# Attention scores in runs of 3, 3 and 2 key tiles, with PSUM banks lent between scores and other products

## The chip, the cores and the metric

The kernel runs on one NeuronCore of a Trainium2 chip. The time is the device time of one execution in microseconds; a kernel is run several times and its median counts. The engines are TensorE (PE, with its weight loads shown apart as PEld), VectorE (DVE), ScalarE (ACT), GpSimd (POOL) and SyncE (SP), which here only issues DMAs. Each engine works through its own queue in order, and the queues meet at semaphores. TensorE writes to PSUM, which has eight banks; a bank holds 512 fp32 numbers in each of 128 partitions, and a [128, 2, 512] tile takes two banks.

## What is computed

Everything is fp32. With x of shape (4, 1024, 1024), a condition of shape (4, 1024) and 16 heads of 64 numbers:

```python
scale, shift = split(cond[:, None, :] @ W_emb + b_emb)
xn = rms_norm(x, g_norm) * (1 + scale) + shift
q, k, v = heads(xn @ W_qkv)                # each (4, 16, 1024, 64)
q, k = rms_norm(q, g_q), rms_norm(k, g_k)
attn = softmax(q @ k.T * 64 ** -0.5)       # over 1024 keys
o = attn @ v
x1 = x + (o + o @ W_out)
y = x1 + causal_conv(x1, taps=cond) + L1_cond_b   # 4 taps along the sequence
```

## The kernel before

**Units.** Attention is cut into 64 units, in the loop `for p in range(B * NB)` at the end of the kernel: a batch (4), a pair of heads (8) and a half of the queries (2 of 512). A unit has eight key tiles of 128 keys. For each tile `scores` multiplies keys and queries for both heads, which lie in the two halves of the PE's rows and run side by side (L688), into a [128, 2, 512] tile `s` of two banks. ScalarE copies it to SBUF as `sp` (L696; the pool of `sp` has nine buffers, so the copy of tile 1 waits until the unit before has used its own tile 0), and VectorE folds it into a running maximum `mx` (L705).

**Softmax of a unit.** `softmax` puts off the following steps by a planner's clock: GpSimd reduces `mx` over the partitions (L710), ScalarE writes the result to a PSUM tile `mbp` (L719), and then for each tile VectorE subtracts it (`shift`, L724), ScalarE takes the exponential and GpSimd adds to a sum (`weigh`, L728 and L730). One unit later `values` multiplies by v (L751, both heads side by side in the PE's columns, into the bank `pav`), and `finish` adds up the denominators (`tot`, L766), which go through DRAM to come back as one reciprocal a row (`spread`, `invert`, L784 to L799), with which `divide` scales the result (L806).

**Pieces.** All other work is a list of pieces for each unit, made by `between(p)`: seven products of the QKV projection (`piece`, L648; each is 8 matmul instructions of 384 columns, fp32 matmuls being issued as two; the projection is done in blocks with 7 products in place of 8, so VectorE adds each product to others when it empties it, L660 to L669), transposes of q and k (`qkt`, L506) and of the next batch's x (`xtp`, L312), and from unit 18 on the output projection of the batch before (`po`, L940, L995, L1009) and the transposes of its results (`otp`, L1056). A piece carries a planned time; `run` calls each, and `tick` moves the planner's clock on and issues what has become due. `need(key)` issues put-off steps of that key at once. What is issued in Python order is each engine's order (`manual_schedule`).

**Where pieces stand.** `split` takes pieces from the end of the list until 26 us of planned time (22 for the first 16 units) are together, to be run behind the unit's last scores; what is left goes into three stretches between the scores:

```python
unit.scores((0, 1))
if last is not None:
    need("exp", last.name)
    last.values(range(0, HT))
fill()
unit.scores((2, 3)); fill(); last.values(range(4, 6)); unit.scores((4, 5))
last.values(range(6, NT)); last.finish(); fill()
unit.scores((6, 7)); need("mx", unit.name); unit.softmax(); fill()
```

Only in units 24, 25, 40 and 41 is the list longer than that, and a timed piece (one QKV product, in 25 and 41 also two transposes) stands between the scores; everywhere else all timed pieces already stand behind the scores.

**PSUM.** The pool `ps_s` has two buffers of two banks for score tiles and `mbp`; `ps_m` has three single banks, taken in turn by every other product and transpose; `ps_a` has one bank for `pav`. That is all eight banks.

Of the kernel before, what the change touches and what calls it, by code (L numbers as in the profile page):

```python
# [21 lines left out]
def kernel(  # L22
# [53 lines left out]
    small = ctx.enter_context(tc.tile_pool(name="small", bufs=2))  # L76
    ps_s = ctx.enter_context(tc.tile_pool(name="ps_s", bufs=2, space=bass.MemoryType.PSUM))
    ps_m = ctx.enter_context(tc.tile_pool(name="ps_m", bufs=3, space=bass.MemoryType.PSUM))
    dram = ctx.enter_context(tc.tile_pool(name="dram", bufs=1, space=bass.MemoryType.DRAM))
# [62 lines left out]

    turn = [0]

    def evacuate(dst, src):

        turn[0] ^= 1
        if turn[0]:
            nc.scalar.copy(dst, src)
        else:  # L150
            nc.vector.tensor_copy(dst, src)

# [23 lines left out]
    for i, g in enumerate((g_q, g_k)):  # L176
        for h in range(2):
            nc.sync.dma_start(rows[R_GQ + i : R_GQ + i + 1, h * D : (h + 1) * D], g.rearrange("(o d) -> o d", o=1))
    cols_ps = ps_m.tile([P, 512], F32, tag="m", name="cols_ps")
    nc.tensor.transpose(cols_ps[:, :NR], rows, ident[:NR, :NR])  # L180
# [83 lines left out]
    class Chunk:  # L264
# [31 lines left out]
        def transposes(self, c):  # L296
            b, k, q = self.b, self.k, self.q
            need("xg", self.name)
            if c == 0:
# [9 lines left out]
                self.stores = [(rs[i // n][:, : min(n, 7 - i), :], i, min(i + n, 7)) for i in range(0, 7, n)]  # L309
            tp = ps_m.tile([P, 2, QN], F32, tag="m", name=f"xtp_{self.name}_{c}")  # L310
            for i in range(4):
# [69 lines left out]
    class Embed:  # L381
# [22 lines left out]
        def run(self):  # L404
            half = self.half
            ps = ps_m.tile([P, 512], F32, tag="m", name=f"mod_ps_{half}")[:, :QN]
            for k in range(NJ):
# [10 lines left out]

            mt = ps_m.tile([P, 512], F32, tag="m", name=f"modT_ps_{half}")[:, :QN]
            mt = mt.rearrange("p (i g b) -> p i g b", i=2, g=4)  # L420
# [27 lines left out]
    class Pair:  # L448
# [51 lines left out]
        def transposes(self, g, s):  # L500

            b, c = self.b, self.c
            need("qk", b, c, g)
            tp = ps_m.tile([P, HN], F32, tag="m", name=f"qkt_{b}_{c}_{g}_{s}")
            for i in range(HT):
                nc.tensor.transpose(  # L506
                    tp[:, i * P : (i + 1) * P], self.qk[g][:, i, s * P : (s + 1) * P], ident
                )
            tag = ("qT", "kT")[s]
            dst = apool.tile([P, HN], F32, tag=f"{tag}{c % 2}{g}", name=f"{tag}_{b}_{c}_{g}", bufs=1)  # L510
            if s:
                nc.scalar.activation(dst, tp, AF.Identity, scale=gqk)
            else:
                nc.scalar.copy(dst, tp)
            (self.qT, self.kT)[s][g] = dst
# [70 lines left out]
    class Double:  # L586
# [39 lines left out]
        def direct(self, c, q):  # L626

            a = self.a[(A11, A12)[c], q] = self.tile_a((A11, A12)[c], q)
            for k in range(KH):
                tp = ps_m.tile([P, 512], F32, tag="m", name=f"xtd_{c}_{q}_{k}")[:, :QN]  # L630
                for i in range(2):
# [6 lines left out]
        def piece(self, i):  # L638

            name, place, t = self.products[i]  # L640
            px, py = self.pairs
            pm = ps_m.tile([P, 512], F32, tag="m", name=f"pqkv_{self.n}_{name}_{t}")[:, :W3]
            w, a = self.w[name], self.a.get((place, t // 2))
# [33 lines left out]
    class Unit:  # L677
# [5 lines left out]
        def scores(self, kts):  # L683
            pr = self.pr
            for kt in kts:
                ps = ps_s.tile([P, 2, HN], F32, tag="s", name=f"s_{self.name}_{kt}")
                for h in range(2):
                    nc.tensor.matmul(  # L688
                        ps[:, h, :],
                        pr.kT[kt // HT][h * D : (h + 1) * D, kt % HT * P : (kt % HT + 1) * P],  # L690
# [4 lines left out]
                sp = apool.tile([P, 2, HN], F32, tag="sp", name=f"sp_{self.name}_{kt}", bufs=9)  # L695
                nc.scalar.copy(sp, ps)  # L696
                self.sp.append(sp)
# [19 lines left out]
        def broadcast(self):  # L717
            mb = ps_s.tile([P, 2, HN], F32, tag="s", name=f"mbp_{self.name}")
            nc.scalar.copy(mb, self.mb)  # L719
# [40 lines left out]
        def finish(self):  # L760
            b, c = self.pr.b, self.pr.c
            tot = ps_m.tile([P, HN], F32, tag="m", name=f"tot_{self.name}")
            for g in range(4):
# [13 lines left out]
            key = ("tot", self.name)  # L777
            defer(0.2, key, lambda: self.spread(tot))
            defer(8.0, key, self.invert)
# [117 lines left out]
    class Quad:  # L897
# [29 lines left out]
        def product(self, name):  # L927
# [9 lines left out]
            else:  # L937
                pm = ps_m.tile([P, 512], F32, tag="m", name=f"po_{b}_{j}_{name}")
            for k in range(KH):
# [23 lines left out]
    class Out:  # L963
# [27 lines left out]
        def residual(self, whole=False):  # L991

            self.pm = ps_m.tile([P, 512], F32, tag="m", name=f"po_{self.name}")
            for i in range(HT):
# [56 lines left out]
        def store(self):  # L1051
            b, j, half = self.b, self.j, self.half
            need("y", self.name)
            tp = ps_m.tile([P, 512], F32, tag="m", name=f"otp_{self.name}")
            for i in range(HT):
# [15 lines left out]
    TO_MAX, TO_SPREAD, TO_SHIFT, TO_EXP, STEP = 2.6, 6.5, 7.6, 1.3, 1.8  # L1071
    BEHIND = 26
    SHARES = (0.25, 0.5, 0.25)
    LEADS = ((11, 7), (10, 9))
    LEADS_LAST = ((11, 7), (10, 12))
    DIVIDE = 18.0
    STEP_FIRST = 1.6
    BEHIND_FIRST = 22.0
    LATER = ((0, 0), (4, 0))
# [174 lines left out]

    def cut(pieces, shares):

        ends = list(accumulate(shares))
        total = sum(t for t, _ in pieces)
        stretches, done = [[] for _ in shares], 0.0
        for t, step in pieces:  # L1260
            at = (done + t / 2) / max(total, 1e-9) * ends[-1]
            stretches[next((i for i, e in enumerate(ends) if at < e), len(ends) - 1)].append((t, step))
            done += t
        return stretches

    def run(pieces):
        for t, step in pieces:
            until = clock[0] + t
            step()
            if until > clock[0]:  # L1270
                tick(until - clock[0])

    def split(pieces, behind):

        left, n = behind, len(pieces)
        while n and left > 0:
            n -= 1
            left -= pieces[n][0]
        return cut(pieces[:n], SHARES) + [pieces[n:]]


# [41 lines left out]
    for p in range(B * NB):  # L1323
        unit = Unit(doubles[p // 4].pairs[p // 2 % 2], p % 2)
        stretches = split(between(p), BEHIND if p >= NB else BEHIND_FIRST)
        if p == B * NB - 1:


            gather(B - 1, 0)
            gather(B - 1, 1)  # L1330
            stretches = cut(between(p), SHARES) + [own]
        stretches = iter(stretches)

        def fill():
            run(next(stretches))

        unit.scores((0, 1))
        if last is not None:
            need("exp", last.name)
            last.values(range(0, HT))  # L1340
        fill()
        unit.scores((2, 3))
        fill()
        if last is not None:
            last.values(range(4, 6))
        unit.scores((4, 5))
        if last is not None:
            last.values(range(6, NT))
            last.finish()
        fill()  # L1350
        unit.scores((6, 7))
        need("mx", unit.name)
        unit.softmax()
        if last is not None:
            defer(2.7 if p > B * NB - 2 else DIVIDE, ("oT", last.pr.b, last.pr.c, last.half), last.divide)
        fill()
        last = unit
# [46 lines left out]
```

## Time and profile before

| what | us |
|---|---|
| median of the timed runs (3) | 2852.54 (2851.46 to 2853.9) |
| span of the profiled execution, first to last instruction | 2846.5 |
| median less span (what lies around the span) | 6.0 |
| PE busy (matmuls) | 2764.2, 97% |
| VectorE, ScalarE, GpSimd busy | 2161.3, 1541.5, 1345.1 |
| QKV products L648 | 1172.5 |
| scores L688, values L751 | 516.3, 486.5 |
| DMA, mean over the span | 179 GB/s |

The profile is of one execution, whose own time around its span is not recorded apart; the span is what its rows add up to. A busy PE counts modelled ends of pipelined matmuls, so the distance from one start to the next says more than a duration. A row of the timeline has the start, the time, the engine, the line, the operation, the tiles (out<-in), the count of merged instructions and, in brackets, the idle time before it and what ended it. A row of the waits has the total idle time, the number of waits and the longest. The clock that was granted to TensorE is 0.995 of full speed over the span.

### The profile page before, as it was taken

What the parts mean: (1) busy time and instruction counts of PE and PEld (TensorE: products, weight loads), DVE (VectorE), ACT (ScalarE), POOL (GpSimd) and SP (SyncE); (2) the same over time, 40 slices, a digit from 0 to 9 for tenths busy, and PEclk for the clock granted to TensorE, in tenths of its full rate; (3) what the DMA queues carried; (4) which work ended last, traced back from release to release, by engine and by line L of the source; (5) the groups of instructions that cost most, each with busy time, mean ns of one, the idle gap of its engine ahead of it and who ended that gap; (6) DMA issues with size and microseconds to landing.
All of it is one profiled execution on the core that took longest, in us unless ns stands there. A gap on an engine that the chain in (4) does not pass through costs nothing.

```text
span 2846.5 us, 31973 instructions
## 1 busy us (share of the span) xinstructions
PE 2764.2 (97%) x10581; PEld 1310.7 (46%) x10581; DVE 2161.3 (76%) x2579; ACT 1541.5 (54%) x2221; POOL 1345.1 (47%) x534
## 2 busy tenths in 40 slices
PE   6999999999999999999999999999999999999998
PEld 3544444444444444444444445445444444443344
DVE  4688887888888777777877777787877877687863
ACT  4255656655555556655555556665555545555532
POOL 2056554565654453553555355355445445554520
PEclk9999999999999999999999999999999999999999
DMA  9844555644565566665565556666556444533334
GB/s 318 280 168 145 193 174 184 211 152 169 174 196 159 174 196 205 214 229 164 162 207 186 165 178 212 203 218 198 163 202 211 141 130 159 167 109 96 118 108 118
DMA packets 416844, 509.40 MB, mean 179 GB/s; under 512 B 40816, under 2 KB 326824, under 8 KB 406952
## 3 DMA queue, kind: packets, MB, share of 16 engines
q1 hardware_dynamic: 416680, 507.36, 55.1%
q8 instruction: 85, 1.39, 0.2%
q14 instruction: 79, 0.65, 0.1%
HBM read 411.85 MB, written 95.40 MB: 178 GB/s over the span
## 4 chain that ended last, share of the span: by engine, by line
PE 78%; DVE 11%; DMA 4%; ACT 3%; issue 2%; POOL 2%; SPq 1%; DVEq 0%; ACTq 0%; POOLq 0%
PE pqkv_P L648 29%; PE pav L751 15%; PE s L688 15%; PE po L1009 5%; PE po_P L940 4%; PE po L940 4%; DVE sp L724 3%; DVE mx L705 3%; POOL sum L730 1%; PE qkt L506 1%; PE tot L766 1%; DMA scrR<-few 1%; DVE qk L498 1%; PE po L995 1%; ACT sp L696 1%
## 5 line engine op out<-in xcount | busy, mean ns | idle before, releaser
L648 PE MATMUL pqkv_P<-w_P,a 128*128 128x384 f32 x3456 | 1172.5, 490 | 15.5 <-issue 5.6
L730 POOL TENSOR_TENSOR sum<-sum,sp 128x1024 f32<-128x1024 f32 x384 | 956.8, 2492 | 36.5 <-ACT sp L728 5.7
L648 PEld LDWEIGHTS pqkv_P<-w_P,a 128*128 128x128 f32 x3456 | 639.4, 190 | 478.7 <-issue 69.2
L696 ACT COPY sp<-s 128x1024 f32<-128x1024 f32 x512 | 506.0, 1015 | 507.4 <-PE s L688 459.1
L705 DVE TENSOR_TENSOR mx<-mx,sp 128x1024 f32<-128x1024 f32 x384 | 518.9, 1351 | 170.9 <-ACT sp L696 143.8
L728 ACT ACTIVATE sp<-sp 128x1024 f32<-128x1024 f32 x512 | 531.8, 1055 | 204.6 <-DVE sp L724 201.3
L724 DVE TENSOR_TENSOR sp<-sp,mbp 128x1024 f32<-128x1024 f32 x512 | 604.2, 1210 | 19.3 <-ACT mbp L719 19.3
L710 POOL PARTITION_ALL_REDUCE mb<-mx x64 | 219.2, 3426 | 826.5 <-DVE mx L705 785.0
L688 PE MATMUL s<-qT,kT 64*128 64x512 f32 x2048 | 516.3, 620 | 21.8 <-DVE sp L724 17.0
L751 PE MATMUL pav<-sp,v 128*64 128x512 f32 x2048 | 486.5, 607 | 0.0
L730 POOL TENSOR_TENSOR sum<-sp,sp 128x1024 f32<-128x1024 f32 x64 | 151.5, 2367 | 485.6 <-ACT sp L728 232.9
L688 PEld LDWEIGHTS s<-qT,kT 64*128 64x128 f32 x2048 | 174.9, 186 | 314.8 <-issue 200.0
L751 PEld LDWEIGHTS pav<-sp,v 128*64 128x64 f32 x2048 | 131.2, 137 | 331.9 <-issue 322.2
L1045 DVE SCALAR_TENSOR_TENSOR y<-x,cols,y 128x512 f32<-128x512 f32 x192 | 224.3, 1173 | 47.9 <-ACT y L1033 43.3
L705 DVE TENSOR_TENSOR mx<-sp,sp 128x1024 f32<-128x1024 f32 x64 | 113.2, 1769 | 102.1 <-ACT sp L696 102.0
L667 DVE TENSOR_TENSOR qk<-u,pqkv_P 128x256 f32<-128x256 f32 x256 | 106.2, 415 | 77.9 <-PE pqkv_P L648 76.5
L1009 PE MATMUL po<-ob,wo 128*128 128x512 f32 x352 | 155.3, 593 | 0.0
L940 PE MATMUL po_P<-o_P,wq_P 128*128 128x512 f32 x320 | 143.9, 592 | 0.0
L498 DVE TENSOR_TENSOR qk<-qk,ms 128x1024 f32<-128x1024 f32 x64 | 129.7, 2047 | 0.0
L719 ACT COPY mbp<-mb 128x1024 f32<-128x1024 f32 x64 | 65.2, 1018 | 111.0 <-POOL mb L710 111.0
L940 PE MATMUL po<-o_P,wq_P 128*128 128x512 f32 x240 | 108.0, 592 | 0.0
L485 ACT ACTIVATE sq<-qk 128x512 f32<-128x512 f32 x128 | 76.7, 627 | 53.6 <-DVE qk L667 53.6
(94 smaller groups left out, 1730.7 us busy)
## 6 DMA issues: line engine op xcount, KB each, us to landing
a<-scrA SPq DMA_DIRECT2D x212, 512.0 KB
w_P<-scrB SPq DMA_DIRECT2D x64, 768.0 KB
o_P<-scrS SPq DMA_DIRECT2D x40, 1024.0 KB
w_P<-in_L_cond_W_qkv_dram SPq DMA_DIRECT2D x192, 192.0 KB
o_P<-scrO SPq DMA_DIRECT2D x30, 1024.0 KB
scrA<-r SPq DMA_DIRECT2D x28, 896.0 KB
wq_P<-scrW SPq DMA_DIRECT2D x70, 256.0 KB
xc<-in_x_dram SPq DMA_DIRECT2D x64, 256.0 KB
```

What stands on the lines that cost most here:

```text
L648: nc.tensor.matmul(pm, (chunk.r(place) if a is None else a[:, k, :])[:, t % 2 * P : (t % 2 + 1) * P], w[:, k, :], start=(k == 0), stop=(k ...
L688: nc.tensor.matmul(ps[:, h, :], pr.kT[kt // HT][h * D : (h + 1) * D, kt % HT * P : (kt % HT + 1) * P], pr.qT[self.half][h * D : (h + 1) * ...
L696: nc.scalar.copy(sp, ps)
L705: nc.vector.tensor_max(self.mx, self.mx if kt > 1 else self.sp[0], self.sp[kt])
L710: nc.gpsimd.partition_all_reduce(self.mb.rearrange("p h q -> p (h q)"), self.mx.rearrange("p h q -> p (h q)"), P, bass_isa.ReduceOp.max,)
L724: nc.vector.tensor_sub(self.sp[kt], self.sp[kt], self.mb)
L728: nc.scalar.activation(sp, sp, AF.Exp)
L730: nc.gpsimd.tensor_tensor(self.sum, self.sum if kt > 1 else self.sp[0], sp, ALU.add)
L751: nc.tensor.matmul(self.pav[h * D : (h + 1) * D, :], self.pr.v[kt // HT][:, kt % HT, h * D : (h + 1) * D], self.sp[kt][:, h, :], start=(kt ...
L940: nc.tensor.matmul(pm, self.w[name][:, k, :], self.o[name][:, k, :], start=(k == 0 and name not in ("P2", "P3", "P4")), stop=(k == KH - 1),)
L1009: nc.tensor.matmul(self.pm, self.w[kh][:, k % KH, :], oTs[b, k, half], start=False, stop=(k == NJ - 1),)
L1045: nc.vector.scalar_tensor_tensor(self.y, self.x1[:, k : k + HN], cols[:, r : r + 1], self.y, ALU.mult, ALU.add)
```

## The change

One pool `psum` with a tag for each bank or bank pair takes the place of `ps_s` and `ps_m`: pairs `s0` and `s1`, single banks `b0`, `b1` and `m`; `pav` keeps its own. Score tile kt uses `s1`, `b0`+`b1`, `s0` in turn; a tile in `b0`+`b1` is copied to SBUF by two ScalarE copies of 512 columns. `mbp` always uses `s0`. Scores are issued in runs of 3, 3 and 2, the values in two runs of 4, `need("exp", ...)` stands ahead of the first scores, and all pieces run behind the last scores. The other products take banks from a list in turn: behind the scores `m, s1, b0, b1` (a pair's first bank is used), during the scores only `m`, ahead of unit 0 also `s0`, and in the last unit without `m`; each change of list starts again at its first entry. `spread` (the copy of `tot` and its DMAs) is issued at once and not 0.2 us of planned time later. `split`, `cut` and the constants BEHIND, SHARES and BEHIND_FIRST go, and an unused helper with them.

```diff
-    ps_s = ctx.enter_context(tc.tile_pool(name="ps_s", bufs=2, space=bass.MemoryType.PSUM))
-    ps_m = ctx.enter_context(tc.tile_pool(name="ps_m", bufs=3, space=bass.MemoryType.PSUM))
+    psum = ctx.enter_context(tc.tile_pool(name="psum", bufs=1, space=bass.MemoryType.PSUM))
...
+    def double_bank(i, name):
+        return psum.tile([P, 2, 512], F32, tag=f"s{i}", name=name)
+    APART = ["m"]
+    FILL = ["m", "s1", "b0", "b1"]
+    ALL = FILL + ["s0"]
+    banks, at_bank = [ALL], [0]
+    def use_banks(some):
+        banks[0], at_bank[0] = some, 0
+    def bank(name):
+        tag = banks[0][at_bank[0] % len(banks[0])]
+        at_bank[0] += 1
+        if tag[0] == "s":
+            return double_bank(int(tag[1]), name)[:, 0, :]
+        return psum.tile([P, 512], F32, tag=tag, name=name)
...
-            pm = ps_m.tile([P, 512], F32, tag="m", name=f"pqkv_{self.n}_{name}_{t}")[:, :W3]
+            pm = bank(f"pqkv_{self.n}_{name}_{t}")[:, :W3]
...
-                ps = ps_s.tile([P, 2, HN], F32, tag="s", name=f"s_{self.name}_{kt}")
+                name = f"s_{self.name}_{kt}"
+                if kt % 3 == 1:
+                    ps = [psum.tile([P, HN], F32, tag=f"b{h}", name=f"{name}_{h}") for h in range(2)]
+                else:
+                    whole = double_bank((kt + 1) % 3, name)
+                    ps = [whole[:, h, :] for h in range(2)]
...
-                nc.scalar.copy(sp, ps)
+                if kt % 3 == 1:
+                    for h in range(2):
+                        nc.scalar.copy(sp[:, h, :], ps[h])
+                else:
+                    nc.scalar.copy(sp, whole)
...
-            mb = ps_s.tile([P, 2, HN], F32, tag="s", name=f"mbp_{self.name}")
+            mb = double_bank(0, f"mbp_{self.name}")
...
-            defer(0.2, key, lambda: self.spread(tot))
+            self.spread(tot)
...
-        stretches = split(between(p), BEHIND if p >= NB else BEHIND_FIRST)
+        pieces = between(p)
...
-            stretches = cut(between(p), SHARES) + [own]
...
-        unit.scores((0, 1))
+            pieces += own
+        use_banks(APART)
         if last is not None:
             need("exp", last.name)
+        unit.scores((0, 1, 2))
+        if last is not None:
             last.values(range(0, HT))
-        fill()
-        unit.scores((2, 3))
-        fill()
+        unit.scores((3, 4, 5))
         if last is not None:
-            last.values(range(4, 6))
-        unit.scores((4, 5))
-        if last is not None:
-            last.values(range(6, NT))
+            last.values(range(HT, NT))
             last.finish()
-        fill()
         unit.scores((6, 7))
+        use_banks(FILL if p < B * NB - 1 else FILL[1:])
         need("mx", unit.name)
         unit.softmax()
...
-        fill()
+        run(pieces)
```

## Prediction, made before the changed kernel was run

> **What bounds the kernel now.** I read the page's busy times first, then the waits of PE, then the timeline of PE and its weight loads through one unit, then VectorE around a unit's start.
>
> ```profile
> PE 2764.2 (97%) x10581; PEld 1310.7 (46%) x10581; DVE 2161.3 (76%) x2579; ACT 1541.5 (54%) x2221; POOL 1345.1 (47%) x534
> ```
>
> PE is busy in 97% of the 2846.5 us span, so a change gains by taking PE time out or by filling the 82 us in which PE is idle. The waits of PE from 130 us on:
>
> ```profile
> PE s L688 <- DVE sp L724: 17.0, 13, 2.2
> PE tot L766 <- POOL sum L730: 6.9, 4, 3.5
> PE pqkv_P L648 <- issue: 5.6, 3, 2.6
> PE s L688 <- ACT sp L696: 4.8, 5, 3.1
> PE pqkv_P L648 <- DVE u L660: 3.3, 4, 1.0
> ```
>
> Scores wait 17.0 us for the subtraction L724 to let go of `mbp`, which shares the two score buffers; the denominators wait for GpSimd's sum; products wait until a bank has been emptied. Busy PE time can shrink only at the seams between kinds of matmul. PE of unit 35, which has no wait:
>
> ```profile
> 1521.82 1.99 PE L688 MATMUL s<-qT,kT 64*128 64x512 f32 x8
> 1523.74 3.65 PE L751 MATMUL pav<-sp,v 128*64 128x512 f32 x16
> 1527.32 1.99 PE L688 MATMUL s<-qT,kT 64*128 64x512 f32 x8
> 1529.24 1.94 PE L751 MATMUL pav<-sp,v 128*64 128x512 f32 x8
> 1531.11 1.99 PE L688 MATMUL s<-qT,kT 64*128 64x512 f32 x8
> ```
>
> and its weight loads, two to a pair of matmuls of the two heads:
>
> ```profile
> 1521.82 0.30 PEld L688 LDWEIGHTS s<-qT,kT 64*128 64x128 f32 x4 [0.55 <-issue]
> 1522.36 0.19 PEld L688 LDWEIGHTS s<-qT,kT 64*128 64x128 f32 x2 [0.23 <-DVE sp L724]
> 1522.79 0.19 PEld L688 LDWEIGHTS s<-qT,kT 64*128 64x128 f32 x2 [0.24 <-issue]
> 1523.74 0.20 PEld L751 LDWEIGHTS pav<-sp,v 128*64 128x64 f32 x4 [0.76 <-issue]
> ```
>
> A pair follows the last after 0.43 us (1522.36 to 1522.79). Two score tiles are four pairs, 4 x 0.43 = 1.72, yet last 1.92 (1521.82 to 1523.74): 0.20 for changing kind. Four more pairs of values cost 3.58 - 1.87 = 1.71; four alone last 1.87: 0.16 for the change. A unit before has four runs of scores and three of values.
>
> **Seams.** After it has three and two: 0.20 + 0.16 = 0.35 less a unit, by single starts in the trace 0.33. Over 63 units 21; the pieces that leave the sections of units 24, 25, 40 and 41 take further seams along, about 1. **-22 us.** These lie on PE itself, so nothing hides them. A section, from first score to last, is then 15.2 and not 15.5, and `tot` stands 12.7 after its start, not 13.1.
>
> **Subtraction and sum.** Before, 18 sections are longer than unit 35's; summed, leaving the last unit out, they lose 31.6 us (starts of score tile 6 against the quiet 13.6). They hold the waits for L724, three of the four for the sum, and three stretches in which PE, after idling 2 to 2.3 us, runs at half clock. Of the first of these (unit 7):
>
> ```profile
> 382.00:387.00 5.00, 4.24 (x12) 1.17 (x14) 2.98 (x6) 4.48 (x8) 4.84 (x3) 0.66 0.96 285
> 1521.00:1537.00 16.00, 16.00 (x75) 5.13 (x73) 11.72 (x14) 9.43 (x13) 9.12 (x4) 1.00 0.46 149
> ```
>
> The column behind POOL's is the granted clock: 0.66 of the 5 us against 1.00. Tile 2 starts 6.3 us after tile 1 there and 4.5 in quiet: 1.8 us a time. After, tiles 0 and 1 have banks of their own, and only tile 2 (`s0`) waits for L724, due 1.8 after the start and not 1.0. With the end of the last L724 after each start (2.2 to 4.3 us in the late units) tile 2 still waits in units 3, 4, 7, 8, 13, 15 to 18: together 9.9 us with unit 61. `tot` comes earlier, but GpSimd's sum does not: in units 2 to 6 it ends 12.7 to 14.7 after the start and PE waits 5.8 us for it. 31.6 - 15.7: **-16 us.** The last unit waits for the same sum (3.54 us) and should gain **-2**, since its exponentials now stand ahead of its score copies in ScalarE's queue.
>
> **The handover, which is new.** Before, scores took `ps_s`, and the last pieces could be emptied at leisure. After, tile 0 needs `s1` and tile 1 `b0` and `b1`, which the last pieces used. Counting the bank calls behind each unit's scores in the order of the code, modulo four, gives the bank of the last piece. With 9 or 13 calls it is `m`: free. With 11 or 12 it is `b0` or `b1`, needed 0.96 after the start; with 10 or 14 it is `s1`, needed at once. In quiet units a QKV product is emptied 0.7 to 1.2 us after the start, so `b0`/`b1` costs 0 to 0.3 and `s1` 0.7 to 1.2. Units 12, 27, 28, 43, 44, 54, 59, 61, 62, 63: 0.9, 0.3, 0.75, 0.3, 0.75, 0.7, 1.2, 1.4, 1.8, 0.45 = 8.6. Dear is the start after every fill that ends with products P4 and P5 and has shift L724 late, here unit 23 (scores at 1010.64):
>
> ```profile
> 1009.87 0.69 DVE L806 TENSOR_TENSOR oT<-pav,rec 128x512 f32<-128x512 f32 x1 [4.10 <-DMA rec<-scrR]
> 1010.48 2.34 DVE L724 TENSOR_TENSOR sp<-sp,mbp 128x1024 f32<-128x1024 f32 x2
> 1012.74 0.41 DVE L667 TENSOR_TENSOR qk<-u,pqkv_P 128x256 f32<-128x256 f32 x1
> 1013.07 0.28 DVE L667 TENSOR_TENSOR v<-u,pqkv_P 128x128 f32<-128x128 f32 x1
> 1013.94 1.28 DVE L491 TENSOR_REDUCE ms<-sq 128x8 f32<-128x512 f32 x2 [0.60 <-ACT sq L485]
> 1015.14 0.41 DVE L667 TENSOR_TENSOR qk<-u,pqkv_P 128x256 f32<-128x256 f32 x1
> 1015.47 0.28 DVE L667 TENSOR_TENSOR v<-u,pqkv_P 128x128 f32<-128x128 f32 x1
> 1015.66 0.55 DVE L669 TENSOR_TENSOR u<-u,pqkv_P 128x384 f32<-128x384 f32 x1
> ```
>
> VectorE stands 4.10 us behind a DMA, then subtracts, then empties the last two products: one (`s1` after) by 2.7, the other (`b0`) by 5.6 after the start. Tile 1 would start at 5.65: 4.7 late. The same reading for units 19, 31, 35, 39, 47, 51 gives 4.2, 2.4, 2.3, 4.0, 1.85, 2.3; with unit 23, 21.8. **+30 us.** Who waits behind tile 1 is all of PE. Bounds: 0, if VectorE comes earlier; and 30 with a half clock after each of the 14 waits of 0.7 us or more (25 more), 55.
>
> Three of the new waits (units 18, 19, 23) leave PE idle over 2.4 us at a stretch, so I add 3 x 1.8: **+5**. The trace shows half clock after idling 1.95, 2.11, 2.25 and 3.06 us, and none after 2.02 and 1.80. The Trainium skill (TensorE: Matmul & The Clock Gate, "Why this matters for your kernels") allows idle gaps up to about 3 us; by that only unit 19 would pay, and this term would be 2. The rows decide.
>
> **Four banks for the pieces.** Behind scores PE idles 19.5 us in all, nearly each time for a bank to be emptied, by at most 2.6 us; a fourth bank gives one product (2.6 us) more. But in units 1 to 17 what a fill gains comes back as a wait for sum or L724. Of 12 there I count 3, of 4 later 3: **-6** (bounds 0 and -19.5). Ahead of unit 0 five banks meet PE's 6 us of waits on VectorE and ScalarE, one of them 3.06 with a half clock behind it; DMAs follow close (1.8 at 71 us): **-1.5** (0 to -8).
>
> **The rest, at nothing.** The copy in halves: 1024 columns take 1015 ns, 512 about 585, so 0.15 more for three tiles a unit; ScalarE is 54% busy and each copy ends before its bank is wanted again. Uncovered it would put off each maximum by 0.15 for tile 7 only: 10 us at most over 64 units if the softmax chain set every unit; it sets about 8, so 1. The early `spread` issues its copy (0.38 us) and five DMAs some 2 us sooner; the reciprocal behind them has its place in VectorE's queue, so `rec` lands no sooner. Loads that stood behind the first scores of some units are issued some 12 us later on SP, where most units have them already, without a DMA wait of PE over 1.8 us; the pieces they serve move too. Unit 0: its scores are bound by ScalarE, -0.3.
>
> **Sum.** -22 - 16 - 2 + 30 + 5 - 6 - 1.5 + 1 - 0.3 = about -12. The span would be 2835; around the span lie 2852.54 - 2846.5 = 6.0 us, which stay: **2841 us**, -0.4%. No change is within 0.2%, 2846.8 to 2858.2, about what a measurement of this kernel can tell.
>
> **Rivals.**
> 1. The handover is hidden: VectorE empties the last pieces sooner, because the DMA that it waits for (4.10 and 2.42 us in units 23 and 31) lands sooner once `spread` goes out earlier. Then +30 +5 become about +8: 2814. For it: that DMA chain starts at `tot`. Against: before scrR stands the reciprocal, which had no wait (at 994.2), and SP's loads.
> 2. Slower: tiles 0 and 1 wait for the last pieces in all 17 units and PE idles long enough to fall to half clock each time. With 55 for the handover in place of 35, and nothing from the fourth bank and ahead of unit 0 (7.5 lost), the sum is +15.5: 2868. It decides once handover and clock together cost over 47. For it: half clock came at 1.95 us of idling. Against: of 17 waits 7 are under 1 us.
> 3. Nothing moves: the chain from the last score (copy, maximum, L710, L719, L724, L728, L730, some 30 us from last copy to last sum) sets more units than the 8 I count, and seams and waits come back before `tot`. 2851. Against: in units 20 to 61 the sum ends 3.5 to 10 after the start, 3 us and more ahead of `tot`.
>
> **Chances.** My forecast 0.50 (its own range 2829 to 2851), rival 1 0.17, rival 2 0.18, rival 3 0.15. Faster by over 0.2%: 0.41 of the forecast's, 0.17 and 0.02, 0.60. Within: 0.09, 0.01 and 0.13, 0.23. Slower: 0.17. The range reaches to rivals 1 and 2: 2814 to 2864.
>
> **What would show it.** Right: the section of a quiet unit 15.2 us, three runs of scores; the 17.0 us of `s` on L724 down to 10; new waits of `s` on L667, L669 and ScalarE's L1033 of some 30 us, the longest about 4.7, in units 19, 23 and 39; fewer waits of `pqkv_P` on VectorE; half clock after the longest. Wrong: no waits on L667 (rival 1), half clock in over ten units (rival 2), more `tot` on L730 (rival 3), or waits of PE on `sp` L696, which would mean that the ring of score banks is too short for ScalarE.

## The result, and the profile after

The changed kernel takes 2898.09 us (median of 5 runs, 2894.31 to 2901.2), the kernel before 2852.54 (5 runs, 2851.46 to 2854.55). The ratio is 1.0158, with a 95% interval of 1.0146 to 1.0171: slower by 1.6%, where 2841 us and a gain of 0.4% were predicted. The profiled executions span 2896.3 and 2846.5 us, 49.8 apart. All sums below are made against these spans. Line numbers are those of the changed kernel from here on: L703 is a score, L743 the subtraction, L658 a QKV product, L673, L677 and L679 its emptying, L785 the denominators, L749 GpSimd's sum.

The busy times of the changed kernel, from its page:

```profile
PE 2760.1 (95%) x10581; PEld 1332.5 (46%) x10581; DVE 2155.2 (74%) x2579; ACT 1560.8 (54%) x2413; POOL 1331.1 (46%) x534
```

PE is busy 4 us less, but idle 136 us and not 82. What it waited for, from the waits of PE over the whole span:

```profile
PE s L703 <- DVE v L677: 21.9, 11, 5.4
PE s L703 <- DVE sp L743: 17.7, 9, 5.9
PE s L703 <- DVE u L673: 13.8, 3, 6.6
PE s L703 <- DVE u L679: 13.7, 10, 3.6
...
PE tot L785 <- POOL sum L749: 6.0, 4, 3.2
PE pqkv_P L658 <- DVE u L670: 5.5, 4, 2.2
```

Three of these rows are new: scores that wait for VectorE to empty a product (L673, L677, L679), 49.4 us. By unit, 23.6 of them stand at the starts of units 25, 26, 41 and 42, 19.7 at the seven starts that the prediction called dear, and 6.1 at the small ones. The waits for the subtraction and for the sum are where they were (17.0 and 6.9 before). Time by groups of units, each from its first score to the next unit's first score, in us against before:

```
units                     what was forecast there          measured
start and unit 0          -1.5 -0.3                         +0.9
1 to 17                   seams, waits, fourth bank: gain   -2.0
18 to 23                  two dear handovers                +8.0
24 to 27, change of batch about -1                         +18.2
28 to 39                  three dear handovers              +6.9
40 to 43, change of batch about -1                         +19.2
44 to 60                  two dear handovers                +2.4
61 to 63                  gain                              -3.7
```

Each profile is of one execution. In units 1 to 17 two kernels with the same instructions there differ by 5.5 us (e2 below and the changed kernel) and by 6.3 us (e5 and the kernel before), so less than that says nothing in this group.

The seams came as forecast. PE in unit 35, whose start is one of the dear ones (1547.80 after, 1521.82 before):

```profile
1547.80 1.13 PE L703 MATMUL s<-qT,kT 64*128 64x512 f32 x4 [1.16 <-DVE v L677]
1549.96 1.99 PE L703 MATMUL s<-qT,kT 64*128 64x512 f32 x8 [1.03 <-DVE u L679]
1551.88 3.65 PE L770 MATMUL pav<-sp,v 128*64 128x512 f32 x16
1555.47 2.85 PE L703 MATMUL s<-qT,kT 64*128 64x512 f32 x12
1558.24 3.65 PE L770 MATMUL pav<-sp,v 128*64 128x512 f32 x16
1561.83 0.64 PE L785 MATMUL tot<-sum,ones 128*32 128x256 f32 x8
1562.40 1.99 PE L703 MATMUL s<-qT,kT 64*128 64x512 f32 x8
```

Behind the second wait the section runs without a gap, in three runs of scores and two of values; a quiet unit's section is 15.2 us and not 15.5. The two waits ahead of it, 1.16 for bank `s1` and 1.03 for `b0`, are the handover.

The large loss is at the changes of batch. VectorE around the start of unit 25:

```profile
1102.68 0.69 DVE L975 TENSOR_TENSOR x<-ou,po 128x512 f32<-128x512 f32 x1 [4.18 <-PE po L959]
1103.28 6.30 DVE L336 TENSOR_TENSOR r<-r 128x256 f32<-128x256 f32 x4
1109.50 2.32 DVE L1064 SCALAR_TENSOR_TENSOR y<-x,cols,y 128x512 f32<-128x512 f32 x3
1111.74 0.41 DVE L677 TENSOR_TENSOR qk<-u,pqkv_P 128x256 f32<-128x256 f32 x1
1112.07 0.28 DVE L677 TENSOR_TENSOR v<-u,pqkv_P 128x128 f32<-128x128 f32 x1
```

and PE in the same stretch:

```profile
1102.47 2.74 PE L658 MATMUL pqkv_P<-w_P,a 128*128 128x384 f32 x8
1105.15 1.98 PE L703 MATMUL s<-qT,kT 64*128 64x512 f32 x6
1112.49 1.23 PE L703 MATMUL s<-qT,kT 64*128 64x512 f32 x2 [5.37 <-DVE v L677]
```

The fill's last product is complete when the scores start at 1105.15. VectorE empties it only at 1111.74, because 9.3 us of other work stand ahead of it in the queue: an addition that empties another product (0.69), and 8.6 us of put-off work, four sums for the next batch's x and three taps of the convolution. The product lies in `b1`, which score tile 1 needs. PE then idles 5.37 us, and the windows view shows the clock granted for what follows (0.50, the number behind POOL's 0.00 (x0)):

```profile
1112.40:1116.00 3.60, 3.50 (x6) 1.19 (x6) 0.00 (x0) 0.00 (x0) 0.00 (x0) 0.50 0.62 174
```

In the kernel before, at the same start (first score at 1099.77), VectorE emptied the product at once and did such sums and taps later (L667 and L326 are that kernel's numbers for L677 and L336):

```profile
1099.94 0.42 DVE L667 TENSOR_TENSOR qk<-u,pqkv_P 128x256 f32<-128x256 f32 x1 [1.96 <-PE pqkv_P L648]
1105.05 1.67 DVE L326 TENSOR_TENSOR r<-r 128x256 f32<-128x256 f32 x4
```

Four sums took 1.67 us there and 6.30 in the changed kernel; the last section says what GpSimd has to do with it.

Why that work stands there is in the planner. `defer_quiet` puts VectorE work off to the end of a window, `loud[1]`, which with the constants of this kernel ends 7.6 + 1.3 + 8 x 1.8 + LOUD 5.0 = 28.3 planned us behind the scores. Before, the fills of units 24, 25, 40 and 41 ended at 26.05 and 26.5 planned us, and no other from batch 1 on, leaving the last out, is longer than 27.8: all end ahead of that date. Now these four have all their pieces, 28.7 planned us in units 24 and 40 and 30.05 in 25 and 41 (added up from the pieces' times in the code), so the date falls inside them. Theory A: the 37.4 us at the changes of batch are this put-off work ahead of an emptying that the next scores wait for, and another 25 are the dear handovers; together they outweigh the seams.

### The profile page after: what moved, and what is told of

Its sections match the earlier page's. It is cut to its first block, busy times and chain, and to the rows that moved or that the text cites. A ratio compares the mean times of both kernels' runs of the same rounds, so it can differ in the third digit from the quotient of the medians.

```text
span 2896.3 us, 32318 instructions
## 1 busy us (share of the span) xinstructions
PE 2760.1 (95%) x10581; PEld 1332.5 (46%) x10581; DVE 2155.2 (74%) x2579; ACT 1560.8 (54%) x2413; POOL 1331.1 (46%) x534
## 4 chain that ended last, share of the span: by engine, by line
PE 67%; DVE 16%; DMA 7%; ACT 3%; issue 3%; POOL 2%; SPq 1%; DVEq 0%; ACTq 0%; POOLq 0%
PE pqkv_P L658 24%; PE pav L770 14%; PE s L703 14%; PE po L1028 5%; DVE mx L724 4%; PE po_P L959 3%; PE po L959 3%; DVE sp L743 3%; DMA scrR<-few 2%; DMA rec<-scrR 2%; POOL sum L749 2%; DVE qk L508 2%; DVE r L336 1%; PE tot L785 1%; PE qkt L516 1%
## 5 line engine op out<-in xcount | busy, mean ns | idle before, releaser
L658 PE MATMUL pqkv_P<-w_P,a 128*128 128x384 f32 x3456 | 1172.6, 490 | 19.9 <-DVE u L670 5.5
L749 POOL TENSOR_TENSOR sum<-sum,sp 128x1024 f32<-128x1024 f32 x384 | 942.2, 2454 | 35.7 <-ACT sp L747 4.4
L658 PEld LDWEIGHTS pqkv_P<-w_P,a 128*128 128x128 f32 x3456 | 641.2, 191 | 479.5 <-issue 71.9
L724 DVE TENSOR_TENSOR mx<-mx,sp 128x1024 f32<-128x1024 f32 x384 | 525.7, 1369 | 144.3 <-ACT sp L715 112.4
L743 DVE TENSOR_TENSOR sp<-sp,mbp 128x1024 f32<-128x1024 f32 x512 | 603.7, 1209 | 33.8 <-ACT mbp L738 33.8
L729 POOL PARTITION_ALL_REDUCE mb<-mx x64 | 219.9, 3436 | 883.5 <-DVE mx L724 846.2
L703 PE MATMUL s<-qT,kT 64*128 64x512 f32 x2048 | 514.9, 626 | 70.3 <-DVE v L677 21.9
L770 PE MATMUL pav<-sp,v 128*64 128x512 f32 x2048 | 477.3, 609 | 0.0
L715 ACT COPY sp<-s 128x1024 f32<-128x1024 f32 x320 | 324.2, 1014 | 255.8 <-PE s L703 210.8
L749 POOL TENSOR_TENSOR sum<-sp,sp 128x1024 f32<-128x1024 f32 x64 | 151.4, 2366 | 492.3 <-ACT sp L747 191.9
L703 PEld LDWEIGHTS s<-qT,kT 64*128 64x128 f32 x2048 | 187.8, 190 | 347.8 <-issue 190.3
L770 PEld LDWEIGHTS pav<-sp,v 128*64 128x64 f32 x2048 | 138.0, 139 | 328.6 <-issue 324.7
L713 ACT COPY sp<-s 128x512 f32<-128x512 f32 x384 | 207.3, 596 | 142.6 <-PE pav L770 139.8
L1064 DVE SCALAR_TENSOR_TENSOR y<-x,cols,y 128x512 f32<-128x512 f32 x192 | 214.4, 1121 | 48.3 <-ACT y L1052 43.8
L724 DVE TENSOR_TENSOR mx<-sp,sp 128x1024 f32<-128x1024 f32 x64 | 110.2, 1722 | 180.2 <-ACT sp L713 164.0
L677 DVE TENSOR_TENSOR qk<-u,pqkv_P 128x256 f32<-128x256 f32 x256 | 105.9, 414 | 69.9 <-PE pqkv_P L658 68.3
```

What stands on the lines that cost most here:

```text
L658: nc.tensor.matmul(pm, (chunk.r(place) if a is None else a[:, k, :])[:, t % 2 * P : (t % 2 + 1) * P], w[:, k, :], start=(k == 0), stop=(k ...
L703: nc.tensor.matmul(ps[h], pr.kT[kt // HT][h * D : (h + 1) * D, kt % HT * P : (kt % HT + 1) * P], pr.qT[self.half][h * D : (h + 1) * D, :], ...
L715: nc.scalar.copy(sp, whole)
L724: nc.vector.tensor_max(self.mx, self.mx if kt > 1 else self.sp[0], self.sp[kt])
L729: nc.gpsimd.partition_all_reduce(self.mb.rearrange("p h q -> p (h q)"), self.mx.rearrange("p h q -> p (h q)"), P, bass_isa.ReduceOp.max,)
L743: nc.vector.tensor_sub(self.sp[kt], self.sp[kt], self.mb)
```

## The experiments

All ratios are against the kernel before, timed on the same chip. Its own median lies between 2849.1 and 2852.5 us in the five groups of runs (the result; e1 to e4; e5 to e8; e9 to e12; e13 and e14), so times of different groups compare no closer than that. A later edit is built on the one named.

**e1: the put-off work later.**

```diff
-    LOUD = 5.0
+    LOUD = 8.0
```

> The changed kernel with one constant, LOUD, at 8.0 instead of 5.0: VectorE work that the planner puts off until the exponentials are done comes due 31.3 planned us after the scores instead of 28.3, so behind the fills of units 24, 25, 40 and 41 (29.6 to 30.1 planned us) and not ahead of their last piece's emptying. Theory A (about 37 us are lost there, because the emptying of a bank that the next scores want stands behind the put-off additions in VectorE's queue): 2862 us, between 2855 and 2872, units 25, 26, 41 and 42 each 6 to 9 us shorter, no wait of the scores above 5 us. Rival B (the loss at the change of batch comes from loads or from the banks alone): 2898 us within 6. Rival C (the put-off work only moves and stalls the next section instead): 2885 to 2905, with new waits behind VectorE in units 25, 26, 41 and 42.

2868.86 us, ratio 1.0054 (1.0036 to 1.0071). (The fills are 28.7 and 30.05 planned us long and not 29.6 to 30.1; both lie between the two dates.) The groups 24 to 27 and 40 to 43 fall from +18.2 and +19.1 to -1.6 each, so 40.5 us are back there; the dear handovers stay and cost 8 us more than before this edit (+9.6, +11.2 and +4.4 in their three groups). Another 5.7 are lost in units 61 to 63, where e6 loses 6.8. Theory A holds for the place; rivals B and C are out.

**e2: in those four units alone the surplus between the scores.**

```diff
+        early = []
+        if p in (24, 25, 40, 41):
+            while sum(t for t, _ in pieces) > 26:
+                early.append(pieces.pop(0))
...
             last.values(range(0, HT))
+        run(early)
         unit.scores((3, 4, 5))
```

> The changed kernel, but in units 24, 25, 40 and 41 alone the first pieces run between the scores of tiles 2 and 3 until 26 planned us are left behind, as before (here through the one bank m). Theory A: the fills end before the put-off VectorE work comes due, so most of the 37 us come back, less some 1 to 2 us per unit for pieces that share one bank: 2863 to 2878 us. Rival B (the bank ring alone costs those units their time): 2893 to 2903. Rival C (those units lose time wherever the surplus stands): above 2890, with the time in the sections of units 24, 25, 40 and 41.

2874.21 us, ratio 1.0079 (1.0063 to 1.0096): the groups become +6.8 and +7.6. By moving the pieces and not the date, 23 of the same 37 us come back. What is left, 3 to 4 us a unit, is more than the 1 to 2 that was expected for pieces sharing one bank.

**e3: the last piece in a bank that no score wants.**

```diff
-    def use_banks(some):
+    def use_banks(some, start=0):
-        banks[0], at_bank[0] = some, 0
+        banks[0], at_bank[0] = some, start
...
-        use_banks(FILL if p < B * NB - 1 else FILL[1:])
+        use_banks(*((FILL, (1 - CALLS[p]) % 4) if p < B * NB - 1 else (FILL[1:],)))
```

`CALLS` is the list of how many banks each unit's fill takes.

> The changed kernel, but each fill begins in the bank of the ring of four that lets its last piece land in m, the bank that no score wants; the three pieces before it land in s1, b0 and b1 in this order. Theory A (the scores wait for the emptying of the fill's last piece): the handovers of the seven dear starts (units 19, 23, 31, 35, 39, 47, 51) and the smaller ones fall away, 20 to 28 us, and 10 to 20 us of the four units at the changes of batch, since only the emptying of the last piece stood wholly behind the put-off work: 2850 to 2868. Rival D (the scores wait for VectorE whatever bank the last piece has, because the next score tile or the softmax wants the same engine): 2888 to 2902. Rival E (the fill's first piece, now in a bank that the scores have only just left, waits as long as the last one did): 2885 to 2900, with new waits of the first piece behind ScalarE's copies.

2854.7 us, ratio 1.0012 (1.0001 to 1.0022): 41 us less than the changed kernel by the spans (2855.6 against 2896.3) and level with the kernel before. Of the 49.4 us that scores waited for an emptying, one wait of 1.0 us is left. The first row of the waits of PE is an old one, the second is the price at the other end of the fill:

```profile
PE s L703 <- DVE sp L743: 21.6, 9, 6.7
PE pqkv_P L658 <- ACT sp L713: 16.8, 18, 1.3
```

The first piece now takes a bank that a score has just left, and waits for ScalarE's copy (with the copies of whole tiles, L715, and the transposes about 27 us). Theory A and rival E are both seen at once; D is out.

**e4: e1 and e3 together.**

> The two edits together: LOUD at 8.0 and each fill's last piece in m. Theory A, if the two losses are separate and add up: 2829 to 2845 us, that is 8 to 23 us below the kernel before, which is the shorter section (0.33 us a unit, 21 us) with little taken back. If the two remedies heal the same stalls: 2850 to 2862. Rival F (the half clock in some stretches, not these waits, makes the rest): 2860 or more.

2855.35 us, ratio 1.0018 (1.0005 to 1.0031), the same as e3 alone. The date of the put-off work and the bank of the last piece are two remedies for one stall: it needs both a late emptying and a score that wants that bank. At the same time e4 loses 5.1 us against e3 in units 61 to 63.

**e7: first and last piece in `m`.** (The fill of unit 60, with six banks, still ends in `b0`.)

```diff
-        use_banks(FILL if p < B * NB - 1 else FILL[1:])
+        use_banks(FILL[:3] * ((1 - CALLS[p]) % 4) + FILL * 5 if p < B * NB - 1 else FILL[1:])
```

> The changed kernel, but each fill both begins and ends in m: the early rounds of the ring leave out b1 as often as is needed for the last piece to land in m. In e3 the fill's first piece stood in s1 or b0, which the scores had just left, and waited 0.3 to 1.3 us for ScalarE's copies in 36 units, 25 us in sum. Theory A (a lent bank costs at both seams of a fill, and m alone costs nothing): those 25 us fall away and nothing else moves: 2826 to 2838 us, faster than the kernel before. Rival G (the fill's first pieces are paced by ScalarE's copies anyway, and the wait passes to the second piece): 2846 to 2858.

2829.48 us, ratio 0.992 (0.9898 to 0.9941): faster than the kernel before. The groups from unit 18 on are +0.2, -3.0, -3.2, -1.4, -5.4 and -2.0, nearly all of it 0.33 us a quiet unit. VectorE at the start of unit 25 is as before this edit:

```profile
1096.69 0.69 DVE L975 TENSOR_TENSOR x<-ou,po 128x512 f32<-128x512 f32 x1 [4.25 <-PE po L959]
1097.29 5.86 DVE L336 TENSOR_TENSOR r<-r 128x256 f32<-128x256 f32 x4
1103.07 2.32 DVE L1064 SCALAR_TENSOR_TENSOR y<-x,cols,y 128x512 f32<-128x512 f32 x3
1105.31 0.41 DVE L677 TENSOR_TENSOR qk<-u,pqkv_P 128x256 f32<-128x256 f32 x1
```

yet PE does not care:

```profile
1096.49 2.74 PE L658 MATMUL pqkv_P<-w_P,a 128*128 128x384 f32 x8
1099.16 2.85 PE L703 MATMUL s<-qT,kT 64*128 64x512 f32 x12
1101.93 3.65 PE L770 MATMUL pav<-sp,v 128*64 128x512 f32 x16
```

The product is emptied 6.15 us after the first score (1105.31 against 1099.16), about as late as in the changed kernel (1111.74 against 1105.15, 6.59), and all three score tiles run without a gap. So the late emptying alone does no harm; it takes a score that wants the bank.

**e8: e7 with LOUD at 8.0.**

> e7 with LOUD at 8.0. e3 and e4 were equal within their intervals, so with the last piece in m it no longer matters where the put-off VectorE work stands: theory A within 4 us of e7, 2826 to 2840 us. Rival H (e4 lost in the last unit what it won at the changes of batch, since there the wait for the subtraction grew to 8.3 us): 6 to 10 us below e7 if that wait does not come back.

2839.55 us, ratio 0.9957 (0.9934 to 0.998), 10 above e7: neither theory expected that. By the spans it is 7.1 us above; 5.2 of them are the last three units (+3.2 against -2.0), 2 are units 18 to 23.

**e5: the kernel before with all pieces behind the scores.**

```diff
-    BEHIND = 26
+    BEHIND = 99
```

> The kernel before with BEHIND at 99: from batch 1 on all pieces of a unit run behind its scores, as in the changed kernel, but with the old banks (two pairs for scores alone, three singles for the pieces) and the old order of scores by twos. Theory A (the put-off work costs only where the scores want a bank that the fill still holds): within 8 us of the kernel before, 2844 to 2860. Rival B' (having all pieces behind the scores costs by itself, since the put-off work and the loads are then late for the pieces): 20 to 37 us slower, 2872 to 2890.

2852.49 us, ratio 1.0006 (0.9994 to 1.0019): no change. The long fills cost 2.5 and 3.1 us in the two groups at the changes of batch, though VectorE is as late at the start of unit 25 (first score at 1093.9) as in the changed kernel (L326, L1045 and L667 are that kernel's numbers for L336, L1064 and L677):

```profile
1092.01 5.92 DVE L326 TENSOR_TENSOR r<-r 128x256 f32<-128x256 f32 x4
1097.85 2.32 DVE L1045 SCALAR_TENSOR_TENSOR y<-x,cols,y 128x512 f32<-128x512 f32 x3
1100.09 0.41 DVE L667 TENSOR_TENSOR qk<-u,pqkv_P 128x256 f32<-128x256 f32 x1
```

The product is emptied 6.2 us after the first score, and since scores have banks of their own there, nobody waits. Rival B' is out.

**e6: the kernel before with LOUD at 8.0.**

> The kernel before with LOUD at 8.0, a control for e1: theory A says that its fills end at 26 planned us, ahead of either date, and that its scores do not share banks with the pieces, so nothing to win: within 5 us of the kernel before. Rival I (a longer quiet stretch is better by itself, with the old banks too): 10 us or more faster.

2854.87 us, ratio 1.0015 (1.0001 to 1.0029). Nothing moves by more than 1.2 us in any group up to unit 60, and the last three units lose 6.8. e1, e4 and e8 lost 5.1 to 5.7 there too.

**e9: scores in runs of 2, 3 and 3 (on e7).**

```diff
-        unit.scores((0, 1, 2))
+        unit.scores((0, 1))
...
-        unit.scores((3, 4, 5))
+        unit.scores((2, 3, 4))
...
-        unit.scores((6, 7))
+        unit.scores((5, 6, 7))
```

> e7 with the scores in runs of 2, 3 and 3 tiles in place of 3, 3 and 2. Tile 2, which needs the bank pair of mbp, then starts 5.5 us after the section's start and not 1.8, behind nearly every last subtraction L743 (it ended 0.8 to 5.0 us after the start in units 1 to 18 of e7). The seams are the same. Theory J (in batch 0 the softmax of the unit before sets the period, so a wait that goes in one place comes back in the next): the waits of the scores for L743 in units 3 to 18 (12.6 us in e7) fall below 3, but the denominators wait longer for the sum, and units 1 to 18 gain less than 5 us: 2822 to 2831 us. Rival K (those waits are time of their own, as the prediction had it): 10 to 13 us there and up to 5 in the last unit: 2811 to 2819.

2833.69 us, ratio 0.9939 (0.9924 to 0.9954), no gain over e7. The waits of the scores for L743 (20.3 us in 11 in e7) vanish from the list, and the next wait takes their place:

```profile
PE tot L785 <- POOL sum L749: 28.5, 12, 9.8
```

In e7 that row is 5.3 us, 3 times. Units 1 to 17 are +0.7 against before, e7 +0.5. The time is 3 us above what theory J gave; the last unit, which waits 9.8 us for the sum, takes 4.4 us more than in e7. But the theory's point is seen: in batch 0 a wait that goes is replaced by the next in the softmax chain.

**e11: four of seven additions of the sum left out in batch 0 (on e7).** The denominators of batch 0 lack four key tiles.

```diff
-            if kt:
+            if kt and (self.pr.b or kt < 4):
                 nc.gpsimd.tensor_tensor(self.sum, self.sum if kt > 1 else self.sp[0], sp, ALU.add)
```

> e7 without four of the seven additions of each unit's denominators on GpSimd in batch 0 (tiles 4 to 7 are left out of the sum there; the other batches are complete). Theory J (GpSimd's sum, at the end of the softmax chain, sets the units in which the denominators wait): all waits for the sum in units 1 to 16 go (5.5 us in e7: units 1, 2, 5, 6), and VectorE, which shares the time with GpSimd, is quicker too: 2818 to 2825 us. Rival N (the sum is not what sets them; once it is gone the same units wait for the subtraction or a product): 2827 to 2833, with those waits in its place.

2810.15 us, ratio 0.9856 (0.984 to 0.9873), 19 us below e7, over three times the waits for the sum that were to be removed. By the end of unit 17 its profiled execution is 24.5 us ahead of that of e7 (which took 4.6 us more than e7's median); no wait for the sum stands among its waits of PE. So GpSimd's sum costs batch 0 more than its waits show. VectorE is quicker too: in units 1 to 16 the running maximum (L724, 112 of them) takes 1.23 us in the mean and 1.72 in e7, 55 us in all, while the subtraction (L743) stays at 1.21. How much of the 19 us comes by way of VectorE was not measured alone.

**e10: loads of the next x later in SP's queue (on e7).** `units[0]` is 0 ahead of unit 0 and 1 from there on.

```diff
-                nc.sync.dma_start(xs, x[self.b, t0 : t0 + P, g * HN : (g + 1) * HN])
-                defer(5.0 + g, ("x", self.name), lambda xs=xs, g=g: self.square(xs, xs, i, g))
+                load = lambda xs=xs, g=g: nc.sync.dma_start(xs, x[self.b, t0 : t0 + P, g * HN : (g + 1) * HN])
+                if units[0]:
+                    defer(3.0, ("x", self.name), load)
+                else:
+                    load()
+                defer(5.0 + 2 * units[0] + g, ("x", self.name), lambda xs=xs, g=g: self.square(xs, xs, i, g))
```

> e7, but the loads of the next batch's x for the row sums are put off by 3 planned us, and their squares on ScalarE by 1 to 2, so that such a load no longer stands in SP's queue ahead of the stores and loads that a product waits for. In the changed kernel one of them stood 7.9 us for ScalarE in unit 6, and the product behind waited 3.6 us (4.0 in e7). Theory M (the order on SP makes that wait and it is time of its own): unit 6 is 4 us shorter and unit 7 keeps its section of 15.7: 2823 to 2828 us. Theory J (softmax sets the period): unit 6 is 4 us shorter and the section of unit 7, which was 3.7 shorter than before, loses as much again: 2827 to 2833.

2826.89 us, ratio 0.9913 (0.9898 to 0.9927), the fastest of the kernels here but e11, which leaves work out; its interval meets that of e7. SP's queue in unit 6 of the changed kernel (start, duration, issue), and the row for its first load from the waits of SP there:

```profile
360.99 0.34 SPq L808 DMA_DIRECT2D few<-scrT  x1
369.32 0.36 SPq L236 DMA_DIRECT2D xs<-in_x_dram  x1
369.78 1.93 SPq L576 DMA_DIRECT2D scrB<-b  x4
371.75 2.60 SPq L615 DMA_DIRECT2D w_P<-in_L_cond_W_qkv_dram  x4
374.40 0.60 SPq L634 DMA_DIRECT2D a<-scrA  x1
...
SPq L236 <- ACT xs L240: 7.9, 1, 7.9
```

The load of `xs` stood 7.9 us for ScalarE to let go of its buffer, and stores and loads stood behind it. In e10 (its lines are 5 further on) it comes last:

```profile
359.00 0.34 SPq L813 DMA_DIRECT2D few<-scrT  x1
365.82 2.10 SPq L581 DMA_DIRECT2D scrB<-b  x4
...
372.48 0.37 SPq L236 DMA_DIRECT2D xs<-in_x_dram  x1
```

Unit 6's fill is 4.4 us shorter than in e7, and unit 7 gives back 0.9. Units 1 to 17 are -9.1 against before, e7 +0.5. Theory M holds in unit 6. The rest of the 9.6 lies mostly in units 1, 8, 9 and 17; its cause stays open, and it is no larger than what two executions with the same instructions differ by there.

**e12: e9 and e10 together.**

> e9 and e10 together: runs of 2, 3 and 3 and the late loads of x. By theory J less than 5 us below e7 in units 1 to 18, and what the last unit gives: 2820 to 2830 us. By K and M together: 2806 to 2815.

2832.66 us, ratio 0.9933 (0.9919 to 0.9948), above both expectations and the same as e9. With runs of 2, 3 and 3 the sum is waited for anyway, and earlier loads give nothing: theories K and M together are out.

**e13: three banks for the pieces (on e10).**

```diff
+    THREE = ["m", "b0", "b1"]
...
-        use_banks(FILL[:3] * ((1 - CALLS[p]) % 4) + FILL * 5 if p < B * NB - 1 else FILL[1:])
+        use_banks(THREE[:2] * ((1 - CALLS[p]) % 3) + THREE * 7 if p < B * NB - 1 else FILL[1:])
```

> e10 (both seams of a fill in m, late loads of x) with three banks for the pieces, m, b0 and b1, in place of four; as there, each fill begins and ends in m. It prices the fourth bank, which the prediction put at 6 us (bounds 0 and 19.5) for the 64 fills. If the step was right: 2830 to 2836 us. If, as the changed kernel's fills say (its waits of products for VectorE did not fall), a product's bank is emptied in time with three as with four: 2824 to 2829. If the fourth bank is what keeps the fills at their length: 2838 and more, with new waits of products for VectorE in most units.

2864.24 us, ratio 1.0048 (1.0033 to 1.0063), 37 above e10 (15 of it in units 1 to 17) and far above what the step and its rival gave. But the edit prices more than it names: to end in `m`, most fills start with rounds of two banks, and in batches 1 to 3 such fills lose 0.4 to 1.4 us each. Among fills without them, units 21, 29 and 33 lose nothing against e10, unit 10 loses 3.2 us, unit 25 3.0 and unit 41 1.3. So the fourth bank is worth something in a few long or early fills; how much of the 37 us is due to the rounds of two stays open.

**e14: the exponentials as before (on e10).**

```diff
-            need("exp", last.name)
-        unit.scores((0, 1, 2))
+        unit.scores((0, 1))
+        if last is not None:
+            need("exp", last.name)
+        unit.scores((2,))
```

> e10 with the remaining exponentials of the unit before issued behind the first two score tiles, as in the kernel before, in place of ahead of them. By the softmax chain (theory J) ScalarE's copies of tiles 0 and 1 go first again, the exponentials end 1 to 2 us later and with them GpSimd's sum: units 1 to 18 and the last unit lose 3 to 8 us: 2830 to 2836. If the place of the exponentials does not matter, because the last exponential waits for VectorE's subtraction anyway: 2824 to 2829.

2827.65 us, ratio 0.9925 (0.9906 to 0.9943), the same as e10. The place of the exponentials is worth nothing that these runs can tell, against the expectation from theory J.

## Why the prediction was wrong, point by point

The span is 61 us longer than forecast. Some 39 of these stand at the changes of batch, 18 are the gains of subtraction and sum that did not come, and the rest is about what the fourth bank was to give.

**Handover, +30: the failed step.** The step counted the bank of the last piece for each unit and then priced seven starts as dear and ten as small. The starts of units 25, 26, 41 and 42 are in neither list and so count as nothing, though the fills ahead of them take 16 and 19 banks and so end in `b1` and `b0`. By the trace of before they look free: the last product ahead of unit 25 is emptied 0.17 us after the first score, in a fill that ended at 26.05 planned us. The sentence on what leaves the sections of units 24, 25, 40 and 41 counted that as "about 1" us of gain and did not ask what the longer fills run into. They are longer than the 28.3 at which `defer_quiet` lets go, which puts 8.6 us (unit 25) and 10.3 us (unit 26) of VectorE work in front of the last emptying. Scores then wait 5.05 to 6.61 us at each of the four starts, and half clock follows. e1 and e7 remove the loss, e2 most of it, and e5 shows that without lent banks it is 2.5 to 3.1 us. That is 37.4 us against a forecast of about -2.

The seven dear starts themselves were right. With 0.33 a unit for the shorter section set aside, the fills ahead of units 19, 23, 31, 35, 39, 47 and 51 and these units' sections grew by 4.8, 4.4, 2.1, 2.5, 6.3, 2.3 and 2.4 us, in sum 24.9; forecast were 21.8 and 5 for the clock. The ten small starts waited 9.2 us in all, 8.6 were forecast. Rival 1 (the handover hidden) is out.

**Clock, +5.** The prediction named units 18, 19 and 23. Half clock followed the waits of units 19, 23 and 39; in unit 18 a wait of 1.88 us was followed by full speed. The rule that the prediction set against its rows (the Trainium skill, TensorE: Matmul & The Clock Gate, "Why this matters for your kernels": no idle gaps above about 3 us) would have spared units 23 and 39 (2.33 and 1.64 us, 2.48 and 1.64); the measurement decides for the rows. The granted clock over the span is 0.985 against 0.995 before: the waits of units 25, 26, 41 and 42 brought four more such stretches, of 6.8 to 10.2 us. So for the waits that it knew of the term was right in number and, but for unit 18, in place.

**Seams, -22.** Right in size: 0.33 us in every quiet unit, by the section of 15.2 us, and e7 keeps it in units 18 to 60. In batch 0 it does not show: units 1 to 17 are -2.0, where seams alone would give -5.6. The next point is the likely reason; it was not shown apart from the rest.

**Subtraction and sum, -16 and -2: wrong.** Rival 3 described it and was set aside for units 20 to 61 only. The changed kernel has the same waits for L743 and L749 as before (17.7 and 6.0 us against 17.0 and 6.9): scores and denominators are asked for sooner, but the softmax chain with GpSimd's sum at its end is no shorter. The last unit gained 0.2 us and not 2: it waits 5.87 us for the subtraction, where it waited 3.09 for a copy of a score tile and 3.54 for the sum. e9 takes one of the two waits away and the other grows by 23 us; e11 shortens the sum and gains 19.

**Fourth bank, -6, and ahead of unit 0, -1.5.** In units 1 to 17 it cannot be told apart from the rest (the fill of unit 6 alone grew by 4.0), the fills of quiet units in e7 are as long as before; the start and unit 0 lost 0.9. e13 shows that the fourth bank is needed in some fills, and doesn't price it alone. That late loads cost nothing fails in unit 6: a load of x that now stands ahead of the stores held up SP for 7.9 us.

**The rest, at nothing.** The copies in halves and the early `spread` left no wait of their own in the trace; e14 says the same for the early exponentials. Rival 2 had the sign and a third of the size, but by another mechanism, half clock after each of 17 waits.

## What to carry to other kernels

When buffers of one stage are lent to another, list for each handover which buffer the last user holds and everything that stands ahead of its release in the releasing engine's queue, in the new order and not in the old trace. A list that is run in turn should begin and end in a buffer that nobody else wants: that alone turned 1.6% slower into 0.8% faster. A planner's dates are part of a change that lengthens a stage past them, and a wait that a chain sets only changes its place.

## What the runs showed of the hardware

Four additions of two [128, 256] operands from SBUF (L336) took 6.30 us in the stretch shown above, where one has a median of 0.42 us (122 in the changed kernel). Two of the four took 2.57 and 2.45 us: the first began 0.13 us and the second 0.24 us after one of GpSimd's sums (2.41 us) had begun, and each ended just after that sum did.

The Trainium skill (SBUF — State Buffer, "SBUF: two separate sides") says that a VectorE instruction with two SBUF inputs and a GpSimd instruction that reads SBUF share a port pair, and that the one that comes second waits for the whole of the other. The two long additions agree. With a GpSimd all-reduce of 3.25 us (L729), an addition that began 0.02 us into it took 2.16 us, but those that began 2.2 us or more into it took 0.42: by these spans, which are rough for such an instruction, the wait ended about 1 us before the all-reduce did.

Half clock followed waits of PE of 5.37 us (unit 25) and 3.59 us (unit 19), and in units 23 and 39 a wait of 2.3 to 2.5 and one of 1.64 us with two matmul pairs between them; waits of 1.16 and 1.03 us (unit 35) were followed by full speed. The length of a wait alone does not decide: after one of 2.48 us in unit 43 the granted clock stayed at 1.00, after one of 2.22 us in unit 13 it fell to 0.50.
